# Attention on one Trainium2 core: the value product in seven-product form beside the query/key product, with one eviction for both, and another order of softmax, mask and attend

## The chip, the core and the metric

The kernel runs on one core of one Trainium2 chip. The metric is the device time in microseconds (us) of one execution; the time given is the median of several. Each profile shows one execution, whose own time is given beside it.

## The reference

`x` is 128 sequences of 64 tokens with 256 features, `adj` is 64 x 64, and all is 32-bit floating point. Four layers follow one another, each of the form `x = x + layer(relu(layernorm(x)))`. Layers 0 (a graph network with an LSTM) and 1 (a graph network with batch norm) aren't touched. The last two are:

```python
# layer 2: three graph parts (diagonal, upper, lower), each with its own 256 x 256 weight
h = einsum('bjf,kfo->kbjo', x, W)
out = einsum('ij,bjo->bio', adj_0, h[0]) + einsum('ij,bjo->bio', adj_1, h[1]) + einsum('ij,bjo->bio', adj_2, h[2]) + bias

# layer 3: causal attention over the 64 tokens of a sequence, one head of 256
q, k, v = split(x @ Wqkv, 3)
scores = einsum('btd,bsd->bts', q, k) / 16 + adj_mask        # adj_mask is adj
scores = where(causal, scores, -1e30)
y = einsum('bts,bsd->btd', softmax(scores), v)
out = y @ Wo
```

## The kernel before, in words

**Data.** The 8192 tokens make 16 blocks of 512 (`NS`, `SUP`), a block is four row tiles of 128 tokens (`Q`), and the 256 features are two chunks of 128 (`KC`). A row tile holds two whole sequences.

**The stage.** Layers 2 and 3 run together in the last fifth of the kernel, block by block: `rest(s, ...)` issues all work of block `s`. Nothing there is scheduled by a planner. Each step is put on a list with a time, `at(t, function, arguments)`; the list is sorted by these times, which are written by hand, and the instructions are issued in that order. [...]the times set nothing but the order on each engine, and the order in which buffers are handed out. Blocks go in pairs: the even and the odd block of pair `i` have their own times, and a pair is planned `PERIOD` = 52.5 after the one before. So even and odd blocks have different neighbours: the odd block's attention runs beside the next even block's graph product.

**The steps of one block**, with the lines of the profile:
- `affine` (L1625, ScalarE) ends layer 1, `turn` (L1641, TensorE) transposes its result and `turned` (L1644, VectorE) adds it to `x`. `norm` gives layernorm and relu: statistics on VectorE (L1655, L1656), the reciprocal root on GpSimd (called POOL in the profile, L1667 to L1670), relu on ScalarE (L1673).
- `graphs3` multiplies with the three parts of `adj` (L1697), in four groups of two PSUM banks; of each group one bank is copied out by ScalarE and one by VectorE (both L1702).
- `gsum` (L1714 to L1720) makes the operand sums on POOL, and `gproduct` (L1730) is the product with the layer's weights in seven-product form (below). `gevict` and `gadd` (L1755, L1758) add it to `x` on VectorE. POOL adds the bias (`biased`, L1685).
- `norm` again, then `h3` (L1765) transposes the result in eight pieces and `h3_copy` (L1769) brings it to SBUF as `h3T`.
- The query and key weights are multiplied together once, ahead of the loop (`weight_product`, the lines from L1575), so that scores need one product per block: `qk = h3T . (Wq Wk^T)`. In the same way `Wv` and `Wo` become one weight, `wvo`. So a block has two products of 512 tokens by 256 by 256: `qk` and the value product `hw`.
- The query/key product is in **seven-product form**: the two feature chunks of the tokens and the two halves of 256 tokens make a 2 x 2 matrix of pieces, the weights another one of 128 x 128 pieces, and 7 products of sums of pieces give the four results in place of 8. `qsum` (L1780, POOL) makes four sums of the data; the sums of the weights (`aqk`) are made once in the first pair by `qk_weights`. `qproduct` (L1793) issues one 256-column matmul for each. Bank `a` collects one product after another (1, 6, 7, 4) and is read out after each; `b` and `c` hold another three. `qcopy` (L1797, ScalarE) copies a bank into a quarter of `qk`, `qadd` (L1800, VectorE) adds one.
- The value product is done directly: `hv` (L1817), eight matmuls of 256 columns into two banks, which `hv_copy` (L1821, ScalarE) copies to `hw`. In the order of TensorE the two products alternate: c2, a1, hv, b5, a6, hv, b3, a7, hv, a4, hv.
- `scores` (L1827), `masked` (L1832, VectorE: scale and mask), `largest` (L1837, VectorE), `exps` (L1840, ScalarE), `turn_e` and `turned_e` (L1848, L1852, L1853: the exponentials transposed and copied), `attend` (L1858) and `attended` (L1863, VectorE: adds to `x`, then SyncE stores the block).
- The last block has nothing behind it to overlap with: `qdirect` (L1807, L1809) and `hv` give both products directly.

**Buffers.** PSUM's eight banks make three pools here: one bank `a`, two banks `bc`, five for everything else, each handed out in turn. A bank is written again when the reader of its last use is done. `qk` lies in `late`, which has one buffer, and `hw` in `pc` with two.

**The first pair** differs: the graph product of block 0 is direct (`gdirect`, L1741), and POOL makes the weight sums of layer 2 (`weight_sum`, L311) and those for attention beside it.

Of the kernel before, what the change touches and what calls it, by code (L numbers as in the profile page):

```python
# [14 lines left out]
P = 128  # L15
# [5 lines left out]
def kernel(ctx: ExitStack, tc: tile.TileContext, a: dict, out: bass.AP):  # L21
# [1276 lines left out]
    with tc.tile_pool(name="pz", bufs=1, reuse_waits="tile") as pz:  # L1298
# [253 lines left out]
        bl2 = row_bcast("bl2", a["bias"], D, late)  # L1552
        wqk = late.tile([P, KC, D], F32, tag="wqk", name="wqk")
        aqk = late.tile([P, 7, P], F32, tag="aqk", name="aqk")
        wvo = late.tile([P, KC, D], F32, tag="wvo", name="wvo")
        wqkv = weight("wqkv", a["Wqkv"], late)
        wo = weight("wo", a["Wo"], late)
# [19 lines left out]
        def weight_product(left, right, to):  # L1577
            p_ = bank().rearrange("p (c m) -> p c m", c=KC)
            for c in range(KC):
                for d in range(KC):  # L1580
                    nc.tensor.matmul(p_[:, c, :], wT[:, left * KC + d, ts(c, P)], right[:, d, :],
                                     start=(d == 0), stop=(d == KC - 1))
            nc.scalar.copy(to, p_)

        weight_product(0, wT[:, KC : 2 * KC, :], wqk)

        def qk_weights(k):
            if k < 4:
                o, c = divmod(k, 2)
                nc.gpsimd.tensor_copy(aqk[:, 2 * o + c, :], wqk[:, c, ts(o, P)])  # L1590
            else:
                weight_sum(aqk, k - 4)

    new_banks(a=1, bc=2, psum=5)
    PERIOD, HALF = 52.5, SUP // 2
    NP = NS // 2
    with tc.tile_pool(name="pc", bufs=2, reuse_waits="tile") as pc, \  # L1600
# [3 lines left out]
        def rest(s, at, only_pair, t_T, t_n, t_G, t_W, t_sums, t_Y, t_relu3, t_h, t_QH, t_S, t_soft, t_E, t_O, end):  # L1604
# [41 lines left out]
            def norm(src, tag, halves, t_rows, t_relu, early=False):  # L1646
# [32 lines left out]
                for k, qs in enumerate((q2s(0), q2s(1)) if halves else (slice(0, Q),)):  # L1679
                    at(t_relu[k] - (6.2 if early else 1.5), root, qs)  # L1680
                    for q in range(qs.start, qs.stop):
                        at(t_relu[k] + 0.6 * (q - qs.start), relu, q)

# [3 lines left out]
            def graphs3(c, k):  # L1687


                if "ag" not in v:  # L1690
                    v["ag"] = pc.tile([P, KC, 3, SUP], F32, tag="ag3", name="ag3")
                half = [bank()[:, : 6 * T].rearrange("p (q k n) -> p q k n", q=2, k=3)
                        for _ in range(2)]
                for q in range(2):
                    for b in range(2):
                        r = slice(b * T, (b + 1) * T)
                        nc.tensor.matmul(half[b][:, q], v["h2"][r, 2 * k + q, ts(c, P)], adj3[r, :, r],  # L1697
                                         start=True, stop=True)
                for b in range(2):
                    copy = nc.vector.tensor_copy if b else nc.scalar.copy  # L1700
                    to = v["ag"][:, c, :, 2 * k * P : (2 * k + 2) * P]
                    copy(to.rearrange("p k (q n) -> p q k n", q=2)[:, :, :, b * T : (b + 1) * T], half[b])  # L1702
# [79 lines left out]

            def c_(o, n):
                return v["qk"][:, o, ts(n, HALF)]

            def qproduct(name, j):
                new = ("q", name) not in v
                if new:
                    v["q", name] = bank("a" if name == "a" else "bc")[:, :HALF]
                if "qk" not in v:  # L1790
                    v["qk"] = late.tile([P, KC, 3 * D], F32, tag="wqkv", name="qk")[:, :, :SUP]
                x_ = (b_(0, 0), b_(1, 0), b_(1, 1), *(v["t"][:, k] for k in (4, 1, 2, 3)))[j - 1]
                nc.tensor.matmul(v["q", name], aqk[:, OF[j], :], x_, start=new,  # L1793
                                 stop=(name, j) in (("a", 4), ("b", 3), ("c", 2)), skip_group_check=True)

            def qcopy(o, n, name):
                nc.scalar.copy(c_(o, n), v["q", name])  # L1797

            def qadd(o, n, name):
                nc.vector.tensor_add(c_(o, n), c_(o, n), v["q", name])  # L1800

            def qdirect(o):
                if o == 0:
                    v["qk"] = late.tile([P, KC, 3 * D], F32, tag="wqkv", name="qk")[:, :, :SUP]
                p_ = bank()
                for c in range(KC):
                    nc.tensor.matmul(p_, wqk[:, c, ts(o, P)], v["h3T"][:, c, :],  # L1807
                                     start=(c == 0), stop=(c == KC - 1))
                nc.scalar.copy(v["qk"][:, o, :], p_)  # L1809

            def hv(q):
                if q == 0:
                    v["hw"] = pc.tile([P, Q, D], F32, tag="hw", name="hw")
                if q % 2 == 0:
                    v["H"] = two(bank())
                for c in range(KC):
                    nc.tensor.matmul(v["H"][:, q % 2, :], v["h3T"][:, c, ts(q, P)], wvo[:, c, :],  # L1817
                                     start=(c == 0), stop=(c == KC - 1))

            def hv_copy(k):  # L1820
                nc.scalar.copy(v["hw"][:, q2s(k)], v["H"])  # L1821

            def scores():
                v["S"] = bank()
                for q in range(Q):
                    for c in range(KC):
                        nc.tensor.matmul(v["S"][:, ts(q, P)], v["qk"][:, c, ts(q, P)],  # L1827
                                         v["h3T"][:, c, ts(q, P)], start=(c == 0), stop=(c == KC - 1))
# [26 lines left out]
            def attend(k):  # L1855
                v["O", k] = two(bank())
                for q in range(2):
                    nc.tensor.matmul(v["O", k][:, q, :], v["eT"][:, ts(2 * k + q, P)],  # L1858
                                     v["hw"][:, 2 * k + q, :], start=True, stop=True)

# [24 lines left out]
            else:  # L1885
                norm("x2", "h2", False, (t_n, t_n + 1.2), (t_n + (4.1 if s == 1 else 8.5 if s % 2 else 7.5),), s % 2 and s > 1)
            for k in range(4):
# [16 lines left out]
            for c in range(KC):  # L1904
                at(t_h + 0.04 * c, h3, c)
                at(t_h + 0.45 * (c + 1), h3_copy, c)
            if not end:
                for k in range(1, 5):
                    at(t_h + 1.1 + 0.35 * k, qsum, k)
                u = 0.43  # L1910
                for k, (name, j) in ((0, ("c", 2)), (1, ("a", 1)), (4, ("b", 5)), (5, ("a", 6)),
                                     (8, ("b", 3)), (9, ("a", 7)), (13, ("a", 4))):
                    at(t_QH + k * u, qproduct, name, j)
                for q, k in enumerate((2, 6, 10, 14)):
                    at(t_QH + k * u, hv, q)
# [28 lines left out]
        for i in range(NP):  # L1944
            t0, first_, end = PERIOD * i, i == 0, i == NP - 1

            def at(t, fn, *args, t0=t0):
# [58 lines left out]
```

## Time and profile before

| | before |
|---|---|
| runs shown, us | 1821.66, 1822.1, 1826.21 |
| median, us | 1822.1 |
| the profiled execution: time, us | 1826.36 |
| the profiled execution: span of the trace, us | 1824.6 |
| clock granted to TensorE | 0.999 |
| ScalarE busy, share of the span | 54% |
| data moved, mean GB/s | 51 |
| 1430 to 1825 us: TensorE, VectorE, POOL, ScalarE busy, us of 395 | 389.0, 247.3, 242.0, 173.1 |

How to read it: the span is the time from the first to the last instruction that the trace shows; the execution's time is a little longer. The profiled execution is one among others, and here it agrees with the slowest of the three runs. The last row is the stretch that holds the stage that is changed: TensorE is busy for nearly all of it. "PE" is TensorE's matmuls, "PEld" its weight loads, which go beside the matmuls, "DVE" VectorE, "ACT" ScalarE, "POOL" GpSimd and "SP" SyncE. A line such as `L1793` is a line of the kernel; names stand as result `<-` operands, and a 32-bit matmul shows as two records, which are called passes below.

### The profile page before, as it was taken

The page shows a single profiled execution, that of the slowest core. Times are in us where ns is not written, and L with a number is a line of the kernel's source. Part 1 is how long each engine was busy: PE and PEld are TensorE (multiplying, and loading weights), DVE is VectorE, ACT ScalarE, POOL GpSimd, SP SyncE. Part 2 cuts the span into 40 slices and gives each one's busy share as a digit, 9 for nine tenths or more (in the row PEclk, how much of TensorE's full clock was granted, in tenths as well). Part 3 has the DMA queues.
Part 4 walks back from the last instruction along what each step waited for, and adds up shares of the span by engine and source line. Part 5 has one row for each costly group of instructions (what it writes and reads, how often), then busy time and mean ns, then how long its engine had stood idle before and what let it go on. Part 6 is the DMA issues. An engine that isn't in the chain of part 4 may idle for free.

```text
span 1824.6 us, 24389 instructions
## 1 busy us (share of the span) xinstructions
PE 1800.3 (99%) x8532; PEld 1299.8 (71%) x8532; DVE 1179.4 (65%) x2346; ACT 988.5 (54%) x1773; POOL 1205.9 (66%) x1215
## 2 busy tenths in 40 slices
PE   8999999999999999999999999999999999999998
PEld 7988444466566887787466666656444899999997
DVE  6875545565566666666556666788876566666664
ACT  6766666644645545544634444687674454444442
POOL 7988454766676777777677776776363666666663
PEclk9999999999999999999999999999999999999999
DMA  6854300000003000003000000433200010111111
GB/s 182 260 169 159 129 0 0 7 1 9 6 24 116 1 1 1 1 1 113 26 0 1 1 1 5 140 125 121 61 1 16 32 47 22 38 47 47 47 47 35
DMA packets 67786, 93.04 MB, mean 51 GB/s; under 512 B 4816, under 2 KB 57808, under 8 KB 67664
## 3 DMA queue, kind: packets, MB, share of 16 engines
q1 hardware_dynamic: 67216, 91.19, 15.0%
q8 instruction: 68, 1.11, 0.3%
q14 instruction: 54, 0.44, 0.1%
q10 hardware_dynamic: 448, 0.30, 0.1%
HBM read 56.99 MB, written 34.47 MB: 50 GB/s over the span
## 4 chain that ended last, share of the span: by engine, by line
PE 92%; POOL 3%; DVE 2%; ACT 2%; issue 2%; DMA 0%; POOLq 0%; DVEq 0%; ACTq 0%
PE ps L983 20%; PE ps L1007 17%; PE ps L875 15%; PE ps L1730 8%; PE ps L1212 5%; PE ps L1457 4%; PE ps L1817 3%; PE ps L463 3%; PE ps L453 3%; PE ps L1697 3%; PE ps L1793 2%; PE ps L492 2%; PE ps L1827 2%; PE ps L1858 1%; PE ps L722 1%
## 5 line engine op out<-in xcount | busy, mean ns | idle before, releaser
L994 DVE TENSOR_TENSOR gate<-gate,ps 128x512 f32<-128x512 f32 (+2 forms) x360 | 216.3, 602 | 184.9 <-PE ps L983 174.0
L1027 ACT ACTIVATE gate<-gate,lbias 128x512 f32<-128x512 f32 (+2 forms) x288 | 175.6, 652 | 171.2 <-DVE gate L994 86.8
L888 DVE TENSOR_TENSOR gate<-gate,ps 128x512 f32<-128x512 f32 (+2 forms) x162 | 100.7, 640 | 129.2 <-PE ps L875 118.9
L992 ACT COPY gate<-ps 128x512 f32<-128x512 f32 (+2 forms) x144 | 74.9, 520 | 155.6 <-PE ps L983 155.1
L875 PE MATMUL ps<-tx,wih 128*128 128x512 f32 (+2 forms) x276 | 117.8, 544 | 1.9 <-ACT gate L891 1.4
L1673 ACT ACTIVATE h<-x,ln_rn 128x256 f32<-128x256 f32 x128 | 68.0, 592 | 92.8 <-POOL ln_rn L1670 92.7
L884 ACT ACTIVATE gate<-gate,lbias 128x512 f32<-128x512 f32 (+2 forms) x108 | 95.8, 887 | 29.1 <-DVE gate L888 29.0
L1730 PE MATMUL ps<-wl,ag 128*128 128x128 f32 x900 | 108.3, 276 | 0.6
L1730 PEld LDWEIGHTS ps<-wl,ag 128*128 128x128 f32 x900 | 104.2, 192 | 3.3 <-ACT ag L1702 2.5
L1037 POOL TENSOR_TENSOR gate<-gate 128x1024 f32<-128x1024 f32 (+4 forms) x41 | 73.8, 1800 | 42.1 <-ACT gate L1027 42.1
L983 PEld LDWEIGHTS ps<-h,wb 128*128 128x128 f32 x392 | 71.1, 190 | 39.6 <-issue 22.0
L1021 DVE TENSOR_TENSOR gate<-gate,ps 128x512 f32<-128x512 f32 (+2 forms) x144 | 80.7, 602 | 22.3 <-PE ps L1007 20.2
L983 PE MATMUL ps<-h,wb 128*128 128x256 f32 (+2 forms) x392 | 91.3, 355 | 0.0
L875 PEld LDWEIGHTS ps<-tx,wih 128*128 128x128 f32 x276 | 51.5, 190 | 55.6 <-issue 39.5
L891 ACT COPY gate<-ps 128x512 f32<-128x512 f32 (+2 forms) x108 | 59.4, 550 | 53.1 <-PE ps L875 52.5
L840 POOL TENSOR_TENSOR tx<-hT 128x512 f32<-128x512 f32 (+2 forms) x29 | 36.0, 1242 | 75.8 <-PE ps L875 73.8
L1040 POOL TENSOR_TENSOR cell<-cell,gate 128x1024 f32<-128x1024 f32 (+2 forms) x36 | 73.0, 2029 | 19.1 <-ACT gate L1027 19.1
L922 POOL TENSOR_TENSOR cell<-gate 128x1024 f32<-128x1024 f32 (+2 forms) x36 | 78.1, 2192 | 5.4 <-ACT gate L884 5.4
L1007 PE MATMUL ps<-hT,wb 128*128 128x512 f32 x160 | 81.7, 592 | 0.0
L1007 PE MATMUL ps<-wih,thA 128*128 128x512 f32 (+2 forms) x192 | 79.3, 495 | 0.0
L875 PE MATMUL ps<-hT,wih 128*128 128x512 f32 (+2 forms) x168 | 78.5, 572 | 0.4 <-DVE h L499 0.4
L1043 POOL TENSOR_TENSOR cell<-cell,gate 128x1024 f32<-128x1024 f32 (+4 forms) x41 | 74.1, 1808 | 3.2
(338 smaller groups left out, 4960.3 us busy)
## 6 DMA issues: line engine op xcount, KB each, us to landing
xt<-in_x_dram SPq DMA_DIRECT2D x30, 512.0 KB, 4.5
x1d<-xt SPq DMA_DIRECT2D x16, 512.0 KB, 2.9
x<-x1d SPq DMA_DIRECT2D x16, 512.0 KB, 4.8
out_dram<-x SPq DMA_DIRECT2D x15, 512.0 KB, 3.4
W<-wb SPq DMA_DIRECT2D x6, 896.0 KB, 4.6
wb<-W SPq DMA_DIRECT2D x6, 896.0 KB, 5.2
wb<-in_WihT_dram SPq DMA_DIRECT2D x32, 128.0 KB, 3.8
wb<-in_WhhT_dram SPq DMA_DIRECT2D x24, 128.0 KB, 3.9
```

Of the source, the lines that this page charges most:

```text
L875: nc.tensor.matmul(wide(p_[:, :N]), wih_of(p, k, gi), x_, start=first_, stop=True, skip_group_check=True)
L884: nc.scalar.activation(to, r[bank_][:, :N] if bank_ else to, fn, bias=lbias[:, l, m : m + 1])
L888: nc.vector.tensor_add(slot(n, hc), slot(n, hc), r[bank_][:, :N])
L922: nc.gpsimd.tensor_mul(cell[:, n, :, :N], i, g_)
L983: nc.tensor.matmul(B[pr, name][:, g * H : (g + 1) * H], w[:, g, :], d, start=(new and g == 0), stop=(name, k) in (("a", 4), ("b", 3), ("c" ...
L992: nc.scalar.copy(to, v)
L994: nc.vector.tensor_add(to, to, v)
L1007: nc.tensor.matmul(to, w, d, start=(pr == 1 and c == 0), stop=(c == 1), skip_group_check=True)
L1021: nc.vector.tensor_add(part(m, k), part(m, k), v)
L1027: nc.scalar.activation(v, v, FN[r, g], bias=lbias[:, l, b : b + 1])
L1212: nc.tensor.matmul(r[name], con["w1"][:, OF[j], g, :], x_, start=new, stop=(name, j) in (("a", 4), ("b", 3), ("c", 2)), skip_group_check=True)
L1730: nc.tensor.matmul(v["g", name][:, p_, :], x_[:, m, ts(p_, P)], wl2[:, OF[j], m, :], start=new and p_ == m == 0, stop=m == 2 and (name, j) ...
```

## The change

The value product of all blocks but the last is made in seven-product form too, on the same four sums of the data. Each of the seven products is now one query/key matmul of 256 columns and two value matmuls of 128 columns, into the two halves of the same PSUM bank (`product` in place of `qproduct` and `hv`). One eviction of 512 columns takes both halves: `copied` four times on ScalarE, `added` three times on VectorE. The value weights get sums of their own, made by POOL in the first pair (`kept_sum`), in a layout that holds the seventh sum in slot 7; the copies of `qk_weights` go, as `weight_product` writes the new layout. `qh` takes the place of `qk` and `hw`, in two buffers that take turns.

The order changes with it. TensorE has the products as a1, b5, a6, c2, a7, b3, a4. In even blocks (but not in the last pair) mask, maximum and exponentials are issued earlier. Around the odd products, TensorE had b3, a7, then hv, the transposes of the next odd block, a4, hv, the turn of the exponentials, scores, attend and the next graph matmuls; it now has b3, the turn of the exponentials, the transposes, a4, attend, scores and the graph matmuls. The odd mask is issued directly after the scores. In the first group of the graph matmuls of even blocks (but the first) both banks are copied by ScalarE. Statistics, root and relu of layer 2 get other times. In the first pair, one weight sum of layer 2 is issued later (19.5 for 17.0), and `h3`, its copies and its sums too.

```diff
--- before.py
+++ after.py
@@ -1550,10 +1550,11 @@
...
-        wqk = late.tile([P, KC, D], F32, tag="wqk", name="wqk")
-        aqk = late.tile([P, 7, P], F32, tag="aqk", name="aqk")
-        wvo = late.tile([P, KC, D], F32, tag="wvo", name="wvo")
-        wqkv = weight("wqkv", a["Wqkv"], late)
+        aqk = late.tile([P, 8, P], F32, tag="aqk", name="aqk")
+        wvo = late.tile([P, 8, P], F32, tag="wvo", name="wvo")
+        wqkv = late.tile([P, 4 * SUP], F32, tag="wqkv", name="wqkv")[:, : 3 * KC * D].rearrange(
+            "p (c m) -> p c m", c=KC)
+        nc.sync.dma_start(wqkv, a["Wqkv"].rearrange("(c p) m -> p c m", p=P))
...
@@ -1580,22 +1581,20 @@
...
-            nc.scalar.copy(to, p_)
-
-        weight_product(0, wT[:, KC : 2 * KC, :], wqk)
-
-        def qk_weights(k):
-            if k < 4:
-                o, c = divmod(k, 2)
-                nc.gpsimd.tensor_copy(aqk[:, 2 * o + c, :], wqk[:, c, ts(o, P)])
-            else:
-                weight_sum(aqk, k - 4)
-
-
-
+            nc.scalar.copy(to, p_ if to.shape[-1] == D else p_.rearrange("p c (o m) -> p c o m", o=KC))
+
+        def blocks(w):
+            return w[:, :4].rearrange("p (o c) m -> p c o m", o=KC)
+
+        weight_product(0, wT[:, KC : 2 * KC, :], blocks(aqk))
+
+        def kept_sum(w, k):
+            op = nc.gpsimd.tensor_sub if k else nc.gpsimd.tensor_add
+            op(*(w[:, m] for m in ((S1, A21, A22), (S2, S1, A11), (7, A11, A21), (S4, A12, S2))[k]))
 
...
     PERIOD, HALF = 52.5, SUP // 2
+    M, SOFT, X, TE, TO = 0.95, 41.0, (2.85, 3.7, 3.75, 3.8), 46.43, (47.5, 47.6, 48.4, 55.4)
...
@@ -1677,9 +1676,9 @@
...
-                    at(t_relu[k] - (6.2 if early else 1.5), root, qs)
+                    at(t_relu[k] - (5.9 if early else 1.5), root, qs)
                     for q in range(qs.start, qs.stop):
-                        at(t_relu[k] + 0.6 * (q - qs.start), relu, q)
+                        at(t_relu[k] + (0.2 if tag == "h2" and s % 2 == 0 and not halves else 0.6) * (q - qs.start), relu, q)
 
...
@@ -1697,7 +1696,7 @@
...
-                    copy = nc.vector.tensor_copy if b else nc.scalar.copy
+                    copy = nc.vector.tensor_copy if b and (c or k or s % 2 or first_) else nc.scalar.copy
                     to = v["ag"][:, c, :, 2 * k * P : (2 * k + 2) * P]
                     copy(to.rearrange("p k (q n) -> p q k n", q=2)[:, :, :, b * T : (b + 1) * T], half[b])
 
@@ -1780,51 +1779,59 @@
...
-            def c_(o, n):
-                return v["qk"][:, o, ts(n, HALF)]
-
-            def qproduct(name, j):
+            def part(c, n, k):
+                return v["qh"][:, c, n, k]
+
+            def new_qh():
+                t = (late if s % 2 else pc1).tile([P, 4 * SUP], F32, tag="wqkv" if s % 2 else "qh", name="qh")
+                v["qh"] = t.rearrange("p (o n k m) -> p o n k m", o=KC, n=2, k=2)
+
+            def product(name, j):
                 new = ("q", name) not in v
                 if new:
-                    v["q", name] = bank("a" if name == "a" else "bc")[:, :HALF]
-                if "qk" not in v:
-                    v["qk"] = late.tile([P, KC, 3 * D], F32, tag="wqkv", name="qk")[:, :, :SUP]
+                    v["q", name] = bank("a" if name == "a" else "bc").rearrange("p (k m) -> p k m", k=2)
                 x_ = (b_(0, 0), b_(1, 0), b_(1, 1), *(v["t"][:, k] for k in (4, 1, 2, 3)))[j - 1]
-                nc.tensor.matmul(v["q", name], aqk[:, OF[j], :], x_, start=new,
-                                 stop=(name, j) in (("a", 4), ("b", 3), ("c", 2)), skip_group_check=True)
-
-            def qcopy(o, n, name):
-                nc.scalar.copy(c_(o, n), v["q", name])
-
-            def qadd(o, n, name):
-                nc.vector.tensor_add(c_(o, n), c_(o, n), v["q", name])
+                last_ = (name, j) in (("a", 4), ("b", 3), ("c", 2))
+                nc.tensor.matmul(v["q", name][:, 0], aqk[:, OF[j] if j < 7 else 7, :], x_, start=new,
+                                 stop=last_, skip_group_check=True)
+                for q in range(2):
+                    nc.tensor.matmul(v["q", name][:, 1, ts(q, P)], x_[:, ts(q, P)], wvo[:, OF[j] if j < 7 else 7, :],
+                                     start=False, stop=last_, skip_group_check=True)
+
+            def copied(o, n, name):
+                if "qh" not in v:
+                    new_qh()
+                nc.scalar.copy(v["qh"][:, o, n], v["q", name])
+
+            def added(o, n, name):
+                nc.vector.tensor_add(v["qh"][:, o, n], v["qh"][:, o, n], v["q", name])
 
...
             def scores():
                 v["S"] = bank()
                 for q in range(Q):
                     for c in range(KC):
-                        nc.tensor.matmul(v["S"][:, ts(q, P)], v["qk"][:, c, ts(q, P)],
+                        nc.tensor.matmul(v["S"][:, ts(q, P)], part(c, q // 2, 0)[:, ts(q % 2, P)],
                                          v["h3T"][:, c, ts(q, P)], start=(c == 0), stop=(c == KC - 1))
 
...
@@ -1855,8 +1862,9 @@
             def attend(k):
                 v["O", k] = two(bank())
                 for q in range(2):
-                    nc.tensor.matmul(v["O", k][:, q, :], v["eT"][:, ts(2 * k + q, P)],
-                                     v["hw"][:, 2 * k + q, :], start=True, stop=True)
+                    nc.tensor.matmul(v["O", k][:, q, :].rearrange("p (o m) -> p o m", o=KC),
+                                     v["eT"][:, ts(2 * k + q, P)], v["qh"][:, :, k, 1, ts(q, P)],
+                                     start=True, stop=True)
 
...
@@ -1883,7 +1891,7 @@
             if first_:
                 norm("x2", "h2", True, (t_T + 0.455, t_T + 1.8), (t_T + 3.2, t_T + 4.6))
             else:
-                norm("x2", "h2", False, (t_n, t_n + 1.2), (t_n + (4.1 if s == 1 else 8.5 if s % 2 else 7.5),), s % 2 and s > 1)
+                norm("x2", "h2", False, (t_n, t_n + (1.75 if s % 2 and s > 1 else 1.2)), (t_n + (4.1 if s == 1 else 8.5 if s % 2 else 7.5),), s % 2 and s > 1)
             for k in range(4):
                 at(t_G + (0.6 if s == 1 else 0.05 if s % 2 else 0.8) * k, graphs3, *((k % 2, k // 2) if first_ else (k // 2, k % 2)))
             if first_:
@@ -1902,26 +1910,18 @@
                     at(t_sums[k], gsum, k)
...
             for c in range(KC):
-                at(t_h + 0.04 * c, h3, c)
-                at(t_h + 0.45 * (c + 1), h3_copy, c)
+                at(t_h + (1.25 if first_ else 0.04) * c, h3, c)
+                at(t_h + (2.55 if first_ and c else 0.45 * (c + 1)), h3_copy, c)
             if not end:
                 for k in range(1, 5):
-                    at(t_h + 1.1 + 0.35 * k, qsum, k)
-                u = 0.43
-                for k, (name, j) in ((0, ("c", 2)), (1, ("a", 1)), (4, ("b", 5)), (5, ("a", 6)),
-                                     (8, ("b", 3)), (9, ("a", 7)), (13, ("a", 4))):
-                    at(t_QH + k * u, qproduct, name, j)
-                for q, k in enumerate((2, 6, 10, 14)):
-                    at(t_QH + k * u, hv, q)
-                at(t_QH + 2 * u, qcopy, 0, 0, "a")
-                at(t_QH + 3 * u, qadd, 0, 0, "c")
-                at(t_QH + 5.1 * u, qcopy, 1, 1, "b")
-                at(t_QH + 6.1 * u, qcopy, 0, 1, "a")
-                at(t_QH + 8 * u, hv_copy, 0)
-                at(t_QH + 10.1 * u, qadd, 1, 1, "a")
-                at(t_QH + 10.2 * u, qadd, 0, 1, "b")
-                at(t_QH + 14.1 * u, qcopy, 1, 0, "a")
-                at(t_QH + 16 * u, hv_copy, 1)
+                    at(t_h + (2.5 if first_ and k > 1 else 1.1) + 0.35 * k, qsum, k)
+                u = 0.88
+                for k, (name, j) in enumerate((("a", 1), ("b", 5), ("a", 6), ("c", 2), ("a", 7), ("b", 3), ("a", 4))):
+                    at(t_QH + k * u, product, name, j)
+                for k, fn, *args in ((1, copied, 0, 0, "a"), (2, copied, 1, 1, "b"), (3, copied, 0, 1, "a"),
+                                     (4, added, 0, 0, "c"), (5, added, 1, 1, "a"), (6, added, 0, 1, "b"),
+                                     (7, copied, 1, 0, "a")):
+                    at(t_QH + k * u + 0.02, fn, *args)
             else:
...
             at(t_S, scores)
-            at(t_S + 2, masked)
+            at(t_S + (2 if only_pair == NP - 1 else 0.1 if s % 2 else M), masked)
             at(t_soft, largest)
             for q in range(Q):
-                at(t_soft + (0.7 if s % 2 or only_pair == NP - 1 else 2.1) + 0.6 * q, exps, q)
+                at(t_soft + (0.7 if s % 2 or only_pair == NP - 1 else X[q]) + (0.6 * q if s % 2 or only_pair == NP - 1 else 0), exps, q)
             for k, qs in enumerate((q2s(0), q2s(1)) if end else (slice(0, Q),)):
                 at(t_E + 0.2 * k, turn_e, qs)
-                at(t_E + 0.2 * k + 0.1, turned_e, qs)
+                at(t_E + 0.2 * k + (0.1 if end else 0.01), turned_e, qs)
...
@@ -1949,13 +1949,15 @@
 
             rest(2 * i, at, i, -8.6 if first_ else -14.5, -12.5, 0,
                  (7.0, 9.6, 12.2, 14.8) if first_ else (7.0, 8.3, 9.6, 10.9, 12.2, 13.5, 15.8),
-                 (3.3, 5.2, 7.1, 9.0), (12.5, 17.5) if first_ else (17.4, 15.3), 20.5, 25.75, 31.4, 40.0, 42.7,
-                 46.3 if end else 48.46, (50.4, 51.26, 51.3, 52.16) if end else (50.85, 51.71, 51.75, 55.4), False)
+                 (3.3, 5.2, 7.1, 9.0), (12.5, 17.5) if first_ else (17.4, 15.3), 20.5, 25.75, 31.4, 40.0, 42.7 if end else SOFT,
+                 46.3 if end else TE, (50.4, 51.26, 51.3, 52.16) if end else TO, False)
             if first_:
-                at(-7.6, weight_product, 2, wo, wvo)
-                at(17.0, weight_sum, wl2, 2)
-                for k in range(8):
-                    at(4 + 0.5 * k, qk_weights, k)
+                at(-7.6, weight_product, 2, wo, blocks(wvo))
+                for k in (0, 1, 2, 3):
+                    at(11.0 + 0.5 * k, kept_sum, wvo, k)
+                at(19.5, weight_sum, wl2, 2)
+                for k in range(4):
+                    at(4 + 0.5 * k, kept_sum, aqk, k)
             rest(2 * i + 1, at, i, -3.0 if first_ else -6.05, 1.5 if first_ else -5.2,
                  12.25 if first_ else 9.0, (17.85, 19.6, 20.9, 22.2, 23.5, 24.8, 26.9),
                  (16.0, 17.0, 18.0, 22.0) if first_ else (12.3, 14.2, 16.1, 22.0), (31.4, 30.6), 35.3, 39.1,
```

More of the change, by code (lines that the diff above doesn't have):

```diff
@@ L1802, in qdirect @@
+            def copied(o, n, name):
[4 more added lines that the diff above has]
+                nc.vector.tensor_add(v["qh"][:, o, n], v["qh"][:, o, n], v["q", name])
             def qdirect(o):
                 if o == 0:
-                    v["qk"] = late.tile([P, KC, 3 * D], F32, tag="wqkv", name="qk")[:, :, :SUP]
+                    new_qh()
                 p_ = bank()
@@ L1806, in qdirect @@
                 for c in range(KC):
-                    nc.tensor.matmul(p_, wqk[:, c, ts(o, P)], v["h3T"][:, c, :],
+                    nc.tensor.matmul(p_, aqk[:, 2 * o + c, :], v["h3T"][:, c, :],
                                      start=(c == 0), stop=(c == KC - 1))
-                nc.scalar.copy(v["qk"][:, o, :], p_)
+                nc.scalar.copy(v["qh"][:, o, :, 0], p_.rearrange("p (n m) -> p n m", n=2))
             def hv(q):
-                if q == 0:
-                    v["hw"] = pc.tile([P, Q, D], F32, tag="hw", name="hw")
@@ L1816, in hv @@
                 for c in range(KC):
-                    nc.tensor.matmul(v["H"][:, q % 2, :], v["h3T"][:, c, ts(q, P)], wvo[:, c, :],
+                    nc.tensor.matmul(v["H"][:, q % 2, :].rearrange("p (o m) -> p o m", o=KC),
+                                     v["h3T"][:, c, ts(q, P)], blocks(wvo)[:, c],
                                      start=(c == 0), stop=(c == KC - 1))
             def hv_copy(k):
-                nc.scalar.copy(v["hw"][:, q2s(k)], v["H"])
+                nc.scalar.copy(v["qh"][:, :, k, 1].rearrange("p o (q m) -> p o q m", q=2),
+                               v["H"].rearrange("p q (o m) -> p o q m", o=KC))
             def scores():
```

## The prediction, made before the changed kernel was run

> **What bounds the kernel now.** I read the page first, then the share of the chain that ended last, then TensorE's waits inside the attention stage, and last single instructions around one evicted bank.
>
> ```profile
> span 1824.6 us, 24389 instructions
> PE 1800.3 (99%) x8532; PEld 1299.8 (71%) x8532; DVE 1179.4 (65%) x2346; ACT 988.5 (54%) x1773; POOL 1205.9 (66%) x1215
> PE 92%; POOL 3%; DVE 2%; ACT 2%; issue 2%; DMA 0%; POOLq 0%; DVEq 0%; ACTq 0%
> ```
>
> TensorE is the bound, and 92% of the chain lies on it. The attention stage (about 1436 to 1822 us) repeats one pair of 512-token blocks. Its period is the distance of equal pieces in the chain: the graph matmuls of L1697 begin at 1668.57 and 1718.28, so 49.71 us. TensorE's waits over the steady pairs (columns: total us, times, longest):
>
> ```profile
> PEld ps L1730 <- ACT ag L1702: 2.5, 7, 0.4
> PEld ps L1697 <- issue: 2.0, 6, 0.3
> PEld ps L1730 <- issue: 1.6, 7, 0.2
> PEld ps L1697 <- ACT ag L1702: 1.4, 7, 0.2
> ```
>
> These are all of them: some 1.1 us of weight-load idling per pair, all at the graph matmuls. Nothing waits in the query/key and value products. So a matmul taken away there is worth its full issue time, and a wait put there costs its full length.
>
> The rate, from the chain (start, length, passes; a 32-bit matmul is two records):
>
> ```profile
> 1684.51 9.38 PE ps L1730 x84
> ...
> 1704.31 0.87 PE ps L1765 x8
> ...
> 1707.84 0.86 PE ps L1817 x4
> ```
>
> A pass of 128 columns goes every 9.38/84 = 0.112 us, a pass of 256 every 0.86/4 = 0.216. One 32-bit matmul is thus 0.223 or 0.432 us.
>
> How a bank is handed back, in the even block's product stream:
>
> ```profile
> 1701.32 0.75 DVE L1800 TENSOR_TENSOR qk<-qk,ps 128x256 f32<-128x256 f32 x2 [1.00 <-PE ps L1793]
> ...
> 1701.85 0.32 PEld L1793 LDWEIGHTS ps<-tq,aqk 128*128 128x128 f32 x2
> ...
> 1701.98 0.38 PE L1793 MATMUL ps<-tq,aqk 128*128 128x256 f32 x1
> ```
>
> The first add (0.42 us) ends at 1701.74; the weight load of the next product into that bank begins at 1701.85, 0.12 later, and its matmul 0.13 after that, just in time. So a hand-back takes 0.12 + 0.11 to 0.13, about 0.23 us. The other direction: the last 128-column pass of a product takes 0.275 us by its record and its reader starts 0.04 later, 0.31 after that pass began (0.09 instead of 0.04 when the reader has a second semaphore to check, as the copy at 1697.92 shows).
>
> **What the Trainium skill says.** "Perfetto Trace Analysis", section on the tensor engine instruction: a matmul's end in the profile is estimated. Agreed here: a 256-column pass is recorded as 379 ns but the next starts after 216, so I price by spacing. "PSUM — Partial Sum Buffer", section on bank collisions: TensorE must not write a bank while another engine reads it, whichever columns; so the value half cannot be written while the query half is copied. The trace has that wait for half-used banks (above). "TensorE: Matmul & The Clock Gate", section on the array's architectural detail: ScalarE and VectorE take instructions strictly in order. The trace agrees: at 1703.94 a copy of L1797 runs after four activations of L1673, although its matmul had ended by 1702.58. "ScalarE: Activation LUTs", section "What ACT_TABLE_LOAD costs": about 1283 ns per load; the trace has one of 1283 ns at L1840.
>
> **The change part by part.**
>
> *Matmuls.* Before, each of 15 blocks has 7 products of 256 columns and 8 value matmuls of 256: 15 x 0.432 = 6.48 us. After: 7 x (0.432 + 2 x 0.223) = 7 x 0.879 = 6.15. Saved 0.325 per block, 4.9 us in all, all on the path. The last block keeps the direct form.
>
> *Evictions.* The four copies grow from 256 to 512 columns and the two value copies go; a 512 copy from PSUM is 0.577 us (L1821), 0.369 before (L1797). The three adds grow to 512: 0.68 us (L1644, same operands' shapes), 0.41 before. Bank "a" has one buffer and takes four products in turn, each read before the next may write. Before, 1.3 us of other matmuls lie between; now one product, 0.879. Take a product as starting at 0: its last pass starts at 0.767, the copy at 1.08, ends 1.66, plus 0.23 is 1.88; the next product into "a" was due at 2 x 0.879 = 1.76. Wait 0.12. So:
> - product 6 waits for the copy after product 1: 0.12 in even blocks, 0.18 in odd ones (that copy checks a second semaphore);
> - product 7 waits for the copy after 6: 0.12;
> - product 4 waits for the add after 7: 1.13 + 0.68 + 0.23 = 2.04 against 1.76, 0.28 in even blocks. In odd blocks a turn of the exponentials and eight transposes (1.3 us) lie between: nothing.
>
> Even 0.53, odd 0.30 us: 8 x 0.53 + 7 x 0.30 = +6.3 us. Everything behind these matmuls on TensorE shifts with them; nobody else is late before. Bounds: the gap is not shown with a 512 copy in this stage. If the hand-back needed only the 0.05 us that a single semaphore takes (the copy ending at 1719.64, load at 1719.69), 0.06 less each; if the restart costs another 0.1, as at 1449.44 after a stall, more by that. I take 0.23 as measured.
>
> *Order of softmax, mask, attend.* Odd scores now follow attend, directly ahead of the even graph matmuls. The second graph group then needs the bank that the mask (0.66 us) reads: 0.2 + 0.66 + 0.05 after the scores, due at about 0.7: 0.2 us late. The first group's two copies both go to ScalarE, the second starting 0.36 after the first; it ends 1.79 after the group's start, where VectorE's ended at 1.55 before. The third group writes that bank, so the first graph product starts 0.24 later. These two overlap: 0.24 per pair, 7 x 0.24 = +1.7 us. Bounds 0 (hidden behind the 0.4 that already stands there) and 0.4. The statistics moved behind the masks let the even maximum end about 1 us sooner, at 1.9 us into the odd products; the exponential placed between two copies then starts at 2.4, and the copy it precedes is due at 3.0, so it costs nothing. If VectorE ran over 0.6 us late it would. POOL's root for the odd block now stands ahead of the graph sums (1.9 us), which have 1.3 us left in hand at their nearest reader, so nothing.
>
> *First pair.* The weight sum leaves the gap between two graph sums: the stall at 1442.43 (0.36) goes. The value weights' four sums (0.46 each) replace four copies and run while TensorE is in the direct products: nothing; if they were late, under 1 us. The exponential's table load stands in ScalarE's order ahead of the copy that product 7 awaits: +1.2, once; bounds 0 and 1.3. Net +0.8.
>
> No DMA moves in SyncE's order; the weight tile's load only gets a longer tile.
>
> Sum: -4.9 + 6.3 + 1.7 + 0.8 = +3.9 us. The profiled execution took 1826.4 us (span 1824.6), 4.3 over the median 1822.1; the runs shown fall at 1821.7, 1822.1 and 1826.2, so such a step is in the spread. The stage's steady period should go from 49.71 to 49.71 - 0.65 + 0.83 + 0.24 = 50.13. I add the sum to the median: 1826.0 us.
>
> **Rivals.**
> 1. *The matmul saving arrives whole.* For it: TensorE runs 99% busy and nothing else bounds. It needs the hand-back under 0.1 us, and the trace shows 0.23. 1822.1 - 4.9 - 0.4 = 1816.8.
> 2. *Slower, through the exponential in ScalarE's order.* In odd blocks it stands between two copies and waits for the maximum, which lies on VectorE behind two transposed adds, two copies, two statistics and the mask. From 0.6 us of lateness on, each tenth goes one for one into product 7. For it: VectorE runs without a pause from the transposed adds to the maximum. Against: that chain, added from its rows, leaves the 0.6. Late by 1.1 us: 7 x 0.5 = 3.5 more, 1829.5.
> 3. *The narrow passes don't keep 0.112 us* once they alternate with wide ones, as a weight load takes 190 ns by its record. L1730 speaks against it. At 0.14: 28 x 0.028 x 15 = +12, near 1838.
>
> **How the numbers follow.** The forecast 0.52, rival 1 0.18, rival 2 0.25, rival 3 0.05. 0.3% (5.5 us) is about what a measurement can tell from no change: faster means under 1816.6, slower over 1827.6. Rival 1 falls at that edge, so half of it and the low end of the forecast, 0.12. Slower: about a quarter of the forecast's spread, most of rival 2 and rival 3, 0.40. Same 0.48. The forecast alone spans 1822 to 1829 from its bounds; without half of the waits (-3) it reaches 1819. Rival 1 below and rival 2 above make it 1816.5 to 1831; rival 3 and the ends of the others are left out.
>
> **What would show it.** Right: in the profile after, TensorE waits at the query/key product for ScalarE's and VectorE's eviction three times an even block and twice an odd one, 0.1 to 0.3 us each; each product takes 0.88; the pair's period is near 50.1. Wrong: no such waits and a period near 49.1 (rival 1), a wait of product 7 above 0.5 (rival 2), a wider spacing of value passes (rival 3).

## The result and the profile after

| | before | after |
|---|---|---|
| median of 15 runs, us | 1821.8 | 1826.62 |
| ratio of the times, 95% interval | | 1.0024 (1.0016 to 1.0033) |
| profiled execution: span, us | 1824.6 | 1825.0 |
| stage: first graph matmul to the end of the span, us | 403.91 | 408.41 |
| of it: up to the second pair's first graph product | 52.20 | 53.96 |
| six steady pairs | 298.27 (49.71 each) | 300.98 (50.16 each) |
| the rest | 53.44 | 53.48 |

The change costs 4.8 us by the medians and 4.50 us in the stage. The spans of the two profiled executions hardly differ, because the stage began at 1420.71 us in one and at 1416.58 in the other: the layers ahead of it, which the change doesn't touch, vary between executions and chips (in the twelve traces of this case the stage begins between 1415.9 and 1422.5). So I read the stage's own length from each trace, one execution of each kernel, and its period, which repeats within 0.01 us from pair to pair.

The page of the changed kernel, its span, its engines and the share of the chain:

```profile
span 1825.0 us, 24766 instructions
PE 1801.8 (99%) x8712; PEld 1308.6 (72%) x8712; DVE 1188.0 (65%) x2339; ACT 989.9 (54%) x1750; POOL 1207.1 (66%) x1215
PE 93%; POOL 2%; ACT 2%; DVE 1%; issue 1%; DMA 0%; DVEq 0%; SPq 0%; POOLq 0%; ACTq 0%
```

TensorE is still 99% busy and carries even more of the chain. Neither line tells that it does less work and takes longer. Its waits over the steady pairs, where three per even block were expected:

```profile
PEld ps L1729 <- issue: 3.9, 13, 0.4
PEld ps L1795 <- issue: 1.3, 6, 0.2
PEld ps L1729 <- POOL tg L1717: 0.2, 1, 0.2
```

At the products (L1795) it lists one wait per even block, the longest, and names "issue", not an eviction. The short ones are too small for it. They stand in the chain, as pieces of the same two passes that take longer than their 0.43 (columns: start, length, passes). Here is the even block's product stream, and below it products 6, 7 and 4 of the odd block:

```profile
1696.40 0.43 PE ps L1795 x2
...
1698.15 0.56 PE ps L1795 x2
...
1700.03 0.56 PE ps L1795 x2
...
1701.91 0.06 issue
1701.98 0.67 PE ps L1795 x2
...
1708.38 0.61 PE ps L1795 x2
...
1710.32 0.56 PE ps L1795 x2
...
1713.51 0.43 PE ps L1795 x2
```

From the top: product 1 needs 0.43; 6 and 7 take 0.56, so 0.13 too much; 4 takes 0.67 and 0.06 of issue, 0.30 too much. In the odd block 6 takes 0.61 and 7 takes 0.56, and 4 is clean. That is 0.56 in an even and 0.31 in an odd block. From pass to pass one sees both parts of a wait: ahead of product 6 the last narrow pass is followed after 0.165 in place of 0.112, and the first wide pass of the product after 0.291 in place of 0.216. Each of these stalls has 0.075 us of restart in it. In the kernel before, the passes of the same stream follow one another after 0.215 to 0.216 us without a break, so that nothing waited there, as the prediction read.

### The profile page after: what moved, and what is told of

Same layout as the page of the kernel before. It is cut to its first block, busy times and chain, and to the rows that moved or that the text cites. A ratio compares the mean times of both kernels' runs of the same rounds, so it can differ in the third digit from the quotient of the medians.

```text
span 1825.0 us, 24766 instructions
## 1 busy us (share of the span) xinstructions
PE 1801.8 (99%) x8712; PEld 1308.6 (72%) x8712; DVE 1188.0 (65%) x2339; ACT 989.9 (54%) x1750; POOL 1207.1 (66%) x1215
## 4 chain that ended last, share of the span: by engine, by line
PE 93%; POOL 2%; ACT 2%; DVE 1%; issue 1%; DMA 0%; DVEq 0%; SPq 0%; POOLq 0%; ACTq 0%
PE ps L983 20%; PE ps L1007 17%; PE ps L875 15%; PE ps L1729 8%; PE ps L1212 5%; PE ps L1457 4%; PE ps L453 3%; PE ps L463 3%; PE ps L1696 3%; PE ps L1795 3%; PE ps L1798 2%; PE ps L492 2%; PE ps L1834 2%; PE ps L1865 1%; PE ps L722 1%
```

## The experiments

Each kernel was profiled; "stage" is the length defined above, of the profiled execution (408.41 for the changed kernel, 403.91 before), "period" that of a steady pair (50.16 and 49.71). Ratios are against runs of the kernel before on the same chip.

**Evictions of half the columns.**
```diff
-                nc.scalar.copy(v["qh"][:, o, n], v["q", name])
+                nc.scalar.copy(v["qh"][:, o, n, 0], v["q", name][:, 0])
-                nc.vector.tensor_add(v["qh"][:, o, n], v["qh"][:, o, n], v["q", name])
+                nc.vector.tensor_add(v["qh"][:, o, n, 0], v["qh"][:, o, n, 0], v["q", name][:, 0])
```

> Leaves out: the value half of each bank is computed but not evicted, and attend multiplies with the query half in its place (the last block as before). So copies are 256 columns (0.37 us for 0.58) and adds 256 (0.41 for 0.68); matmuls, their order and their number are those of the changed kernel. Theory (the banks' hand-back is the cost): all waits ahead of products 6, 7 and 4 vanish, 0.87 us a pair in the six steady pairs and about 0.6 in each outer one, so 6.4 less than the changed kernel's 1826.6: 1820.2, and a steady period of 50.16 - 0.87 = 49.29. Rival (the waits are only where TensorE pays for something else, the new order or POOL's sums): the waits turn up at another line and the time stays within 1 us of 1826.6.

Measured: period 49.34, stage 402.83, ratio 0.9994 (0.9986 to 1.0002). Evictions, from the groups by form (mean ns of one behind the comma):

```profile
L1804 ACT COPY qh<-ps 128x256 f32<-128x256 f32 x48 | 17.7, 370 | 58.5 <-PE ps L1798 57.9
L1807 DVE TENSOR_TENSOR qh<-qh,ps 128x256 f32<-128x256 f32 x36 | 15.1, 419 | 16.0 <-PE ps L1798 16.0
```

With 370 ns for 584 and 419 for 686, and the same matmuls, no product waits: 0.82 us a pair come back, of 0.87. The last pair gained only 0.04: there the transposes of L1764 then wait twice 0.38 us for ScalarE's relu, as one of them did before the change. So the stage fell by 5.6, not 6.4.

**Either half of the change alone.** First the new products with the old order, then the old products with the new order.
```diff
-    M, SOFT, X, TE, TO = 0.95, 41.0, (2.85, 3.7, 3.75, 3.8), 46.43, (47.5, 47.6, 48.4, 55.4)
+    M, SOFT, X, TE, TO = 2, 42.7, (2.1, 2.7, 3.3, 3.9), 48.46, (50.85, 51.71, 51.75, 55.4)
...
-                    at(t_QH + k * u, product, name, j)
+                    at(t_QH + (4.5 / u if s % 2 and s > 1 and k == 6 else k) * u, product, name, j)
```

> The new products with the softmax, mask, attend and copy order of the kernel before (one half of the odd block's transposes stands ahead of product 4, the other behind it, so that neither product 4 nor the scores wait). Theory: the bank waits stay (0.56 in even and 0.31 in odd blocks), the 0.25 us at the graph matmuls goes in each pair, and the exponential no longer stands between two copies in the first pair (1.3): 1826.6 - 7 x 0.25 - 1.3 = 1823.6, steady period 49.9. Rival (the new order is what costs, the products are a gain): the matmul saving arrives whole, 1821.8 - 4.9 = 1816.9, period 49.05.

Measured: period 51.51, stage 415.78, ratio 1.0062 (1.0050 to 1.0075). Neither theory had this. The bank waits were there and the graph matmuls were faster, but attend waited:

```profile
PEld ps L1865 <- DVE eT L1859: 6.8, 6, 1.2
...
PEld ps L1834 <- DVE qh L1807: 2.0, 6, 0.8
```

The first line is attend waiting for VectorE's copy of the turned exponentials, the second the scores waiting for an add. Both stand on VectorE behind the add for a transpose that I had put behind product 4. So the edit was mended:
```diff
-                    at(t_QH + (4.5 / u if s % 2 and s > 1 and k == 6 else k) * u, product, name, j)
+                    at(t_QH + k * u, product, name, j)
```

> As e2_old_order, but with both transposes of the odd block ahead of product 4, as in the kernel before; in e2_old_order one of them stood behind product 4, and VectorE's add for it held up the copy of the turned exponentials. Theory: that misplacement made e2's 1.2 us wait at attend; without it the bank waits stay (0.87 a pair), the graph matmuls lose nothing, and the scores wait about 0.3 for the copy of product 4, which has only the turn of the exponentials (0.44) ahead of it: period 50.2, stage (first graph matmul to the end) about 407, 3 us above the 403.9 of the kernel before. Rival (the old order doesn't fit the new products at all, as VectorE's 512-column adds crowd out the copy of the exponentials): attend still waits over 0.8 us, period above 51.

Measured: period 50.79, stage 411.46, ratio 1.0036 (1.0023 to 1.0049). In its waits the same two lines of TensorE have become:

```profile
PEld ps L1865 <- DVE eT L1859: 3.2, 6, 0.5
...
PEld ps L1834 <- ACT qh L1804: 1.2, 6, 0.2
```

The misplacement made half of the wait, but attend still waits 0.5 us a pair for the copy of the exponentials, and the scores 0.2 for the copy of product 4. So the theory's period of 50.2 is missed, and the rival is half right: VectorE is late for that copy in the old order. Its last product add (0.68 us) now runs between the adds for the transposes and three row tiles' statistics, and the copy comes behind all of them; in the kernel before, that add took 0.41 and ran ahead of the adds for the transposes. No run separates the add's length from its place.

Next the old products with the new order. The edit to the kernel before is the change without its product lines and those of the first pair; only the attends are 0.5 later, behind the last value matmul:
```diff
+    M, SOFT, X, TE, TO = 0.95, 41.0, (2.85, 3.7, 3.75, 3.8), 46.43, (48.05, 48.1, 48.4, 55.4)
...
-                    copy = nc.vector.tensor_copy if b else nc.scalar.copy
+                    copy = nc.vector.tensor_copy if b and (c or k or s % 2 or first_) else nc.scalar.copy
```

> The kernel before with only the new order of softmax, mask, attend, statistics and copies; its products, evictions and buffers stay. Theory: no bank waits and no matmul saving; the graph matmuls lose 0.25 us in each of seven pairs and the table load may hold a copy once (0 to 1.3): 1823.6 to 1824.9, steady period 49.96. Rival (the new order is what costs): 1826 or more, period above 50.1.

Measured: period 49.97, stage 405.93, ratio 1.0014 (1.0007 to 1.0020), as the theory had it. So the new order costs the old products 0.26 us a pair, but saves the new ones 0.63 (50.79 to 50.16). And between this kernel and the one with half evictions, which has the same order and no bank waits, lies the matmul saving by itself: 49.97 - 49.34 = 0.63 a pair, for 0.65 in the prediction.

**The table load put where ScalarE idles.**
```diff
+                at(30.0, nc.scalar.activation, late.tile([P, 1], F32, tag="warm", name="warm"), mone[:, :1], AF.Exp)
```

> The changed kernel with one more activation of one column with the exponential, issued in the first pair where ScalarE idles, so that the table load stands there. Theory: the wait of 1.4 us ahead of product 7 in the first odd block falls to its usual 0.13, all of it on the path: 1826.6 - 1.27 = 1825.3. Rival (the graph matmuls that follow wait for POOL's or VectorE's work of the first pair anyway): 1826.6, with the wait moved to the graph matmuls.

In the changed kernel the chain of the first odd block runs through it:

```profile
1456.33 0.59 ACT qh L1804
...
1456.94 1.28 ACT L1847
...
1458.54 0.19 ACT sc L1847
1458.73 0.48 ACT qh L1804
...
1459.34 0.67 PE ps L1795 x2
```

Copy after product 1, table load, one exponential, copy after product 6, and only then product 7. With the load issued earlier, the first part of the stage went from 53.96 to 52.69, 1.27 less, period unchanged, stage 407.32, ratio 1.0021 (1.0013 to 1.0029). The theory held.

**Other work between two products into one bank.** The transposes that stood behind the products go between them.
```diff
-                    at(t_T + 0.1 * k, turn, k)
-                at(t_T + (1.5 * k if first_ else 7.5 + 0.1 * k if seam else 0.1 * k) + 0.01, turned, k)
+                    at(t_T + (0.1 * k if s < 3 else (-2.75, -1.0)[k] if s % 2 else (-3.15, -1.4)[k]), turn, k)
+                at(t_T + (1.5 * k if first_ else 7.5 + 0.1 * k if seam else 0.1 * k - (0 if s < 3 or s % 2 else 1.2)) + 0.01, turned, k)
```

> The changed kernel with the next block's transposes (two groups of four, 0.44 us each) moved into the gaps of the product stream: in odd blocks one ahead of product 6 and one ahead of product 7, in even blocks one ahead of product 7 and one ahead of product 4. Their adds on VectorE stay where they were, or behind the product adds. Nothing is added or taken away. Theory (a bank wait is a lack of other work between two products into one bank): 0.13 + 0.30 of the even block's 0.56 and all 0.31 of the odd block's go; period 50.16 - 0.74 = 49.42, stage 408.4 - 4.7 = 403.7, level with the kernel before. Rival (the eviction time itself is on the path, whatever lies between): period within 0.2 of 50.16.

Measured: period 49.60, stage 404.34, ratio 0.9997 (0.9988 to 1.0006). All waits that had got other work are gone, 0.74 us a pair, but 0.17 came back at attend: only product 4 (0.88) now lies between the turn of the exponentials and attend, which needs VectorE's copy of them.

> e5_fillers with the table load of e4_early_table. Theory: the two gains are in different places and add up: 1.27 less than e5_fillers, stage 402.4, 1.5 us under the kernel before. Rival: the wait of the first odd block is filled by the moved transposes already, and it stays at e5's time.

Measured: first part 52.61 for 53.26, period 49.60, stage 403.70, ratio 0.9999 (0.9990 to 1.0007). Between the two: 0.65, not 1.27, as the transposes ahead of product 7 already covered half of the load's wait. The gains overlap in that one place.

**The graph matmuls.** First try, on top of the last kernel: the copy back on VectorE, with one row tile's statistics ahead of the mask and one far behind, and POOL's root after it.
```diff
-                    copy = nc.vector.tensor_copy if b and (c or k or s % 2 or first_) else nc.scalar.copy
+                    copy = nc.vector.tensor_copy if b else nc.scalar.copy
...
-                    at(t_rows[q // 2] + 0.6 * (q % 2), stats, q)
+                    at(t_rows[q // 2] + (4.4 if early and q == 3 else 0.6 * (q % 2)), stats, q)
```

> e6_fillers_table with the second copy of the first graph group back on VectorE, and the odd block's statistics of the last two row tiles moved away from it (one ahead of the mask, one behind the second group's copy; POOL's root follows). Theory (three copies in a row on ScalarE are what makes the third and fourth graph group late): 0.2 of the 0.25 us a pair come back, period 49.2, stage 402.4 - 1.4 = 401.0, 2.9 under the kernel before. Rival (VectorE is late there whatever the order, as the mask runs first): no gain or up to 0.3 a pair lost.

Measured: period 50.54, stage 410.59, ratio 1.0027 (1.0016 to 1.0039): slower by 0.94 a pair. Its chain goes from the late statistics to POOL's root, which relu and the next graph group wait for:

```profile
1669.34 0.56 DVE ag L1701
1669.90 0.34 DVE ln_st L1654
...
1670.81 1.03 POOL ln_rn L1667
```

I had looked for what VectorE is late for, and not for who waits for the statistics that I moved. Second try: VectorE's adds for the odd block's transposes use its idle time among the products, so that all statistics fit ahead of the mask.
```diff
-                at(t_T + (1.5 * k if first_ else 7.5 + 0.1 * k if seam else 0.1 * k - (0 if s < 3 or s % 2 else 1.2)) + 0.01, turned, k)
+                at(t_T + (1.5 * k if first_ else 7.5 + 0.1 * k if seam else 0.1 * k if s < 3 else (-0.95, -0.45)[k] if s % 2 else 0.1 * k - 1.2) + 0.01, turned, k)
...
-                    copy = nc.vector.tensor_copy if b and (c or k or s % 2 or first_) else nc.scalar.copy
+                    copy = nc.vector.tensor_copy if b else nc.scalar.copy
...
-                norm("x2", "h2", False, (t_n, t_n + (1.75 if s % 2 and s > 1 else 1.2)), (t_n + (4.1 if s == 1 else 8.5 if s % 2 else 7.5),), s % 2 and s > 1)
+                norm("x2", "h2", False, (t_n, t_n + (0.3 if s % 2 and s > 1 else 1.2)), (t_n + (4.1 if s == 1 else 8.5 if s % 2 else 7.5),), s % 2 and s > 1)
```

> e6_fillers_table; now VectorE's adds for the odd block's transposes follow these in its idle time among the product adds, so that all four statistics come ahead of the mask; with VectorE free after the mask, the second copy of the first graph group goes back to it from ScalarE. Theory (three copies in a row on ScalarE make the third and fourth graph group late): the 0.25 us a pair come back, period 49.60 - 0.25 = 49.35, stage 403.7 - 1.7 = 402.0. Rival (the mask so close to the graph matmuls is what makes them late, through the bank it reads): period stays at 49.6 or above.

Measured: period 49.38, stage 402.02, ratio 0.9995 (0.9987 to 1.0004). 0.22 of the 0.25 came back. The trace shows where: in the kernel without this edit the first group's second copy, on ScalarE, ends 1.81 us after the group's first matmul, and the third group's matmuls into its bank follow at 1.86. Back on VectorE it ends at 1.55, and they follow at 1.61. The mask begins 0.11 after the group's first matmul in both, so the copies behind one another were the cause, not the mask's bank.

**The turn of the exponentials one product earlier**, ahead of product 3.
```diff
-    M, SOFT, X, TE, TO = 0.95, 41.0, (2.85, 3.7, 3.75, 3.8), 46.43, (47.5, 47.6, 48.4, 55.4)
+    M, SOFT, X, TE, TO = 0.95, 41.0, (2.85, 3.7, 3.75, 3.8), 46.38, (47.5, 47.6, 48.4, 55.4)
-                at(t_E + 0.2 * k + (0.1 if end else 0.01), turned_e, qs)
+                at(t_E + 0.2 * k + (0.1 if end else 0.05), turned_e, qs)
```

> e9_graph_copy with the turn of the even block's exponentials one product earlier (ahead of product 3 in place of product 4). In e5 and e6 attend waited 0.17 us for VectorE's copy of the turned exponentials, as only product 4 lay between. Theory: that wait goes and nothing takes its place, period 49.35 - 0.17 = 49.18, stage 402.0 - 1.2 = 400.8, 3.1 us under the 403.9 of the kernel before; against its runs 1821.8 - 3 = 1818.8. Rival (the exponentials aren't ready by then): TensorE waits at the turn in place of attend, no gain.

Measured: period 49.20, stage 400.82, 1823.74 us against 1825.53 on the same chip, ratio 0.9989 (0.9981 to 0.9998). It is the only version that is faster than the kernel before beyond its interval, and only just; it keeps all of the change's matmuls. The stage is 3.09 us shorter, as expected; the medians differ by 1.79, and the interval, some 0.4 to 3.5 us, holds both. Its even block, in the chain:

```profile
1696.90 0.56 PE ps L1795 x2
...
1698.78 0.44 PE ps L1640 x4
1699.22 0.43 PE ps L1795 x2
...
1700.97 0.44 PE ps L1640 x4
1701.41 0.43 PE ps L1795 x2
```

Only product 6 still takes 0.56. Products 7 and 4, with four transposes (L1640) ahead of each, are back at 0.43.

## Why the prediction was right, step by step

The forecast was 1826.0 us, the result is 1826.62; in the stage, +3.9 was forecast and +4.50 measured. The miss of 0.6 is made of 0.54 in the first part, 0.2 in the six steady pairs and -0.16 at the end.

- **Matmuls**, 0.65 a pair: right, 0.63 between two kernels that differ in it.
- **Bank waits**, 0.53 and 0.30 us: right, 0.56 and 0.31. The saving did arrive, and was eaten by waits that the change itself made: a copy grew from 0.37 to 0.58 us and an add from 0.41 to 0.69, while the other matmuls between two uses of the bank shrank from 1.3 us to one product of 0.88. That the size fits so well is partly luck: the second half of the assumed hand-back is not where the prediction had it (last section). The half evictions and the moved transposes take these waits away in two independent ways. Where the prediction would look for them was wrong: the view of waits shows one of the five in a pair, and the chain shows all.
- **Order**, 0.24 a pair: right in size and place. The old products with the new order pay 0.26, and moving the copy back gives 0.22. What the prediction missed is why the order is needed: its old form costs the new products 0.63 more a pair, most of it through VectorE.
- **Exponential in ScalarE's order** (rival 2): not late in steady pairs, as the forecast had it; product 7 waits 0.13, not above 0.5. The table load cost 1.27, for 1.2.
- **First pair**, net +0.8: this step failed. The first part of the stage lost 1.76; by the prediction's terms it should have been -0.65 + 0.53 + 0.30 + 0.24 + 0.8 = 1.22. The stall at 1442.43 (0.36) did go: POOL's sum is in time now. But the change opens another, which the prediction put at nothing. It issues half of the transposes of `h3` later, so that only four instead of eight are left ahead of the last graph product into bank `a`; the other four stand ahead of product 1, where c2 stood. With so little in between, that graph product waits for VectorE's add, as the query/key products do: 0.40 us at 1442.83, restart included, where nothing waited before (lines below). This is most of the 0.54. It was read from the traces, and no run undid it alone.
- **Last pair**, +0.2 by the terms: +0.04. Waits at the products took the place of a wait for relu that was there before.

The last graph product of the first pair and the transposes ahead of it, first in the kernel before, then in the changed one:

```profile
1446.55 1.04 PE L1765 MATMUL ps<-ident,h 128*128 128x128 f32 x8
1447.42 1.50 PE L1730 MATMUL ps<-wl,ag 128*128 128x128 f32 x12
...
1442.06 0.60 PE L1764 MATMUL ps<-ident,h 128*128 128x128 f32 x4
1442.26 0.42 DVE L1757 TENSOR_TENSOR x<-x,ps 128x256 f32<-128x256 f32 x1 [0.92 <-PE ps L1729]
...
1442.83 0.57 PE L1729 MATMUL ps<-wl,ag 128*128 128x128 f32 x3 [0.17 <-DVE x L1757]
```

Rival 1 (the saving arrives whole) fell to the waits, rival 3 (narrow passes) to their spacing: 0.109 to 0.112 us between wide ones. What the prediction says of half-used banks, that a bank must not be written while other columns of it are read, no run here shows: each product first writes the very columns that the eviction reads.

## What to carry to other kernels

When a change merges outputs into one bank, compare three numbers: the eviction that is now longer, its hand-back on both sides, and the matmul time between two uses of that bank; here waits of 0.13 to 0.30 us at five of a pair's fourteen products turned a gain of 0.65 a pair into a loss. The cure was not a faster eviction but other work of TensorE put between the products, and VectorE's work moved into its idle time. And where instructions are moved away, look for who needed them where they stood: twice here a wait came from that, at the bank that the moved transposes had covered (the first pair) and at the root that needs the moved statistics.

## What was not expected of the hardware

A stalled product pays in two places: 0.05 to 0.23 us more until its first pass, and 0.075 more between its first two passes (0.291 for 0.216). Of the 0.128 us that products 6 and 7 lose in even blocks, the second is more than half.

The prediction had the hand-back as 0.12 us from the end of the eviction to the weight load and another 0.11 to 0.13 to the matmul. Ahead of product 6 the copy ends at 1697.896 and the load begins at 1698.010, which is 0.114; but the first pass follows 0.030 later, and 0.075 comes behind it. Together that is 0.22 for the assumed 0.23. The 0.13 had been read at 1701.98, where the matmul wasn't stalled at all (its pass comes 0.216 after the one before), so it could not show what a stalled one pays. Whether the 0.075 is the rest of the weight load or something else, no run here shows.
